# A graph network layer on one core: sorted-table quads closer together, the last node blocks two steps apart, a norm one step later, and a memset on another engine

## The chip, the cores and the metric

The kernel runs on one core of a Trainium2 chip. Its engines work side by side, each through its own list of instructions in order: TensorE (PE) multiplies, VectorE (DVE) and ScalarE (ACT) work on elements, GpSimd (POOL) issues the gathers and scatters whose rows are named by an index (indirect DMAs), SyncE (SP) issues the plain DMAs. They meet at semaphores. The metric is the time of one execution on the device in microseconds (us), the median of several runs; lower is better.

## The reference, cut to what matters

Three layers of message passing over 6250 nodes with 256 features and 100000 edges of three types, in single precision. The edges come sorted by their destination, which is denser at low node numbers. Each edge has 32 attributes, which one matrix turns into its weights; these serve all three layers.

```
ew = edge_attr @ edge_w + edge_b
inv_cnt[i] = 1 / max(number of edges of type i into the node, 1)
for l in range(3):
    residual = x
    msg = relu(x[src] * ew)
    out = 0
    for i in range(3):
        h = segment_sum(msg * (edge_type == i), dst) * inv_cnt[i]
        out = out + h @ weights[l, i]
    out = out + x @ roots[l] + biases[l]
    x = residual + relu(out)
result = layernorm(x_in + x)
```

## The kernel before, in words

The edges are cut into tiles of 128; two tiles are a pair, two pairs a quad. There are 391 pairs. The nodes are cut into 49 blocks of 128 (the last has 106). The names of the blocks are 0 to 48.

Each layer is one list of steps, written out by the function `layer`, whose loop over `it` emits for every step the instructions of several stages, each for a pair that lies some steps ahead. The schedule is manual: what stands earlier in this loop stands earlier in the list of its engine. The list of layer 0 has 391 steps, those of layers 1 and 2 have 414. A step `it` does:

- `gather` (line 1422, POOL): two indirect DMAs fetch the source rows of the pair of step `it + 9` into a quad buffer `xs`, of which there are 8;
- `reduce` (lines 881, 884, 892, PE): the messages of the pair of step `it` are multiplied with one-hot matrices (destination by type) and summed up in a bank of PSUM, `h_p`; `add` (line 932, DVE) later adds a finished bank to the accumulator `acc`;
- `make_ew` (line 820, PE; layer 0 only): the edge weights of the quad five steps ahead, into a PSUM buffer `ew_p`;
- `keep_ew` (layer 0 only): ACT copies the weights of the quad four steps ahead into one of three buffers `keep`. For most quads (line 776) SP writes them to memory for the later layers;
- `weigh` (line 843 on DVE, line 844 on ACT): product of the rows and their weights, then the relu, for the quad three steps ahead;
- the end of a node block (below), and in layer 2 its norm.

**The sorted table.** The first 52 pairs of edges (26 quads) go to a few nodes. In layer 0 their weights are not kept in order: each row is scattered to a place in a table in memory (`zone_table`), sorted by source block and type, from which the later layers read them with plain loads and without a gather. For these quads `keep_ew` (line 770) leaves the four tiles in a list `waiting`, and `gather_pair` calls `scatter` (line 733) after each of its gathers as long as that list has entries. So POOL's list has four scatters between gathers soon after each such quad, and the first of them waits for the copy of line 770. At which steps these quads stand is set by `places_of`: near `ZONE_AT + int(ZONE_SPACE * j)` for quad number j, counted in pairs of the list, rounded up to an even pair. The same places cut the sums of `reduce` (`spans_of`).

**The end of a block.** The function `schedule` gives each block c a step `starts[c]` once all of its sums are there. Blocks 2 to 48 come in this order, with block 0 among them; block 1 is the last of all. Most blocks take two steps per part, the last five (44 to 48, `QUICK = 5`) one step per part (`paces`). With s the start of one of those five: at step s `node_mul` (line 961, PE) multiplies the first type's sum with its weights into the PSUM buffer `o_p`; at s + 1 `node_end` (lines 988 to 992, DVE) adds that to `x_root`, and `node_mul` does the other two types; at s + 2 `node_end` adds those, makes the new rows (line 995) and SP writes them to memory (line 998, `x_mid`), and ACT clears the sums (line 978). There is one buffer `o_p`, so a matmul into it waits until DVE has read the one before. Within a step `node_end` stands ahead of `node_mul`.

**From layer to layer.** The first 6 pairs of the next layer (12 gathers, `gather_early`) are put in POOL's list at steps 388 to 393 of layer 0 and 411 to 416 of layer 1, behind all other gathers of the layer. They read `x_mid`, which block 48's write completes; block 1 is left out of them and added later (`complete`, line 835).

**The norm** (layer 2). When a block is over at step o, `node_end` also makes its mean and variance in `mv` (lines 1001 and 1003, DVE; two buffers each). `deviate` (line 1007, ACT) takes the root at o + 1; `norm` at o + 2 takes the reciprocal (1012) and a product (1013) on DVE, scales the rows on ACT (1014) and writes them out (1015, SP; ACT for block 1).

**Columns of ones.** The quad buffers `xs` have a 257th column of ones, with which line 881 counts edges while it sums. Line 517 sets it once, for all 8 buffers, before layer 0.

Of the kernel before, what the change touches and what calls it, by code (L numbers as in the profile page):

```python
# [442 lines left out]
def ordered_path(ctx, tc, x, attr_laid, A, weights, roots, biases, edge_w, edge_b, out, src, src_i, seg, place_i, consts, x_root,  # L443
# [6 lines left out]
    nc = tc.nc  # L450
    P = 128
    N, D = x.shape
    E = src.shape[0]
    L, R = weights.shape[:2]
    NT = (N + P - 1) // P
# [58 lines left out]

    edge = ctx.enter_context(tc.tile_pool(name="edge", bufs=2))
    all_rows = big.tile([P, ROWS, 2, 2, D + 1], F32, name="xs")
    nc.vector.memset(all_rows.rearrange("p n k i d -> p (n k i) d")[:, :, D:], 1.0)
    rooms = [all_rows[:, n] for n in range(ROWS)]
    wpool = ctx.enter_context(tc.tile_pool(name="wpool", bufs=1))
    o_pool = ctx.enter_context(tc.tile_pool(name="o_p", bufs=1, space=PSUM))  # L520
# [163 lines left out]
    def layer(l, r_sb, b_sb, ats, early, pools):  # L684
# [4 lines left out]
        order, starts, moved, _, _ = schedule(N, E, share, l)  # L689
# [15 lines left out]
        def first_of(p, n):  # L705
            return p == 0 or order[p - 1] // n != order[p] // n
# [302 lines left out]
        def norm(c):  # L1009
            n = min(P, N - c * P)  # L1010
            mv = mvs[c]
            nc.vector.reciprocal(mv[:n, 1:2], mv[:n, 2:3])
            nc.vector.scalar_tensor_tensor(mv[:n, 0:1], mv[:n, 0:1], -1.0, mv[:n, 1:2], op0=ALU.mult, op1=ALU.mult)
            nc.scalar.activation(x_all[:n, c, :], x_all[:n, c, :], AF.Identity, bias=mv[:n, 0:1], scale=mv[:n, 1:2])
            (nc.scalar if c == 1 else nc.sync).dma_start(out[c * P:c * P + n, :], x_all[:n, c, :])
# [10 lines left out]
        over_at = {s + 2 * paces(c, NT): c for s, c in node_at.items()}  # L1026
# [5 lines left out]
        for j, c in enumerate(turns_of):  # L1032
            step = max(3 + int((steps - 110) * (1 - (1 - j / NT) ** 0.5)), max(root_at, default=-1) + 6)
            if j >= roots_in:
                step = max(step, starts[turns_of[j - roots_in]] + 5)
            assert step + 8 <= starts[c]
            root_at[step] = c
        if l > 0:
            for p, u in enumerate(order):
                if u >= ZU:  # L1040
                    _, b, n = lots[u // 2 - ZU // 2]
# [3 lines left out]
        if l == L - 1:  # L1045
            used = {c: s + 1 for s, c in root_at.items()}
            used[1] = max(used[1], FIRST + 1)
            for p, u in enumerate(order):
                if u >= ZU:
                    _, b, n = lots[u // 2 - ZU // 2]  # L1050
                    used.update((c, max(used[c], p - 3)) for c in range(b, b + n))
            for c in turns_of:
                step = max(used[c], max(given_at, default=0) + 2)
                assert step <= starts[c] + 2, (c, step, starts[c])
                given_at[step] = c
        for it in range(-11, max(starts) + 8):
            it_is[0] = it
            def pair(k):
                return order[it + k] if 0 <= it + k < steps else None
# [26 lines left out]
            if l == L - 1 and it in given_at:  # L1086
                c = given_at[it]
# [21 lines left out]
            if pair(3) is not None and pair(3) // 2 == order[-1] // 2:  # L1109
                k = pair(3) % 2  # L1110
# [36 lines left out]
                    node_mul(1, 2)  # L1147
            if it - 1 in over_at and l == L - 1:
                deviate(over_at[it - 1])
            if it - 2 in over_at and l == L - 1:  # L1150
                norm(over_at[it - 2])
            if pair(2) is not None and first_of(it + 2, 2) and pair(2) // 2 != order[-1] // 2:
                one_hot(pair(2) // 2)
            if pair(3) is not None and first_of(it + 3, 2) and pair(3) // 2 == order[-1] // 2:
# [40 lines left out]
SORT_AT = 4  # L1195
SORT_EVERY = 6
ZONE_AT = 114
ZONE_SPACE = 7.5
MIDDLE_AT = 12
LOT_AT = 6  # L1200
LOT_SPACE = 4.5
# [1 line left out]
QUICK = 5  # L1203
# [48 lines left out]
def places_of(N, E):  # L1252

    K = first_pairs(N, E)
    quads = [K + ZONE_AT + int(ZONE_SPACE * j) for j in range(zone_of(N, E) // 2)]
    lots = [K + LOT_AT + int(LOT_SPACE * j + LOT_MORE * j * j) for j in range(len(lots_of(N)))]
# [96 lines left out]
def paces(c, NT):  # L1353

    return 1 if c >= NT - QUICK else 2


def schedule(N, E, share, l):

    P = 128  # L1360
    U = -(-E // (2 * P))
    NT = -(-N // P)
    K = first_pairs(N, E)
    last = last_pairs(N, E)
    spans = spans_in(N, E, l)
    order = order_of(N, E, l)
    added = {s: p + 1 for s, p in stages(N, E, share, l)[2].items()}
    done = []
    for c in range(NT):
        edges = E * min(1.0, (P * (c + 1) / N) ** 0.5)  # L1370
        u = U if c == NT - 1 else min(U, -(-int(edges) // (2 * P)) + 4)
        done.append(max(added[s] for s in spans if K <= s[0] < U and (s[0] < u or s[0] == K)))
    node = lambda e: int(N * min(1.0, max(0.0, e / E)) ** 2)
    least = [node(2 * P * u - ASTRAY) for u in range(U)]
    most = [node(2 * P * u + ASTRAY) for u in range(U)]
    for u in range(last, U):
        least[u] = max(least[u], P)
    moved = done[1] + 1
    ready = max(added[s] for s in spans if s[0] < last or s[0] >= U) + 2
    starts = [None] * NT  # L1380
    step = moved
    for c in range(2, NT):
        if starts[0] is None and ready <= max(done[c] + 2, step + 4):
            step = starts[0] = max(ready, step + 4)
        step = starts[c] = max(done[c] + paces(c, NT), step + 2 + paces(max(c - 1, 2), NT))
    if starts[0] is None:
        step = starts[0] = max(ready, step + 4)
    starts[1] = max(max(added.values()), step + 4)

    for s in spans:  # L1390
        u, p = s[0], added[s]
        if u >= U:
            assert p <= starts[0]
        elif u >= K:
            assert all(p <= starts[c] or least[u] >= P * (c + 1) for c in range(2, NT))
            assert p <= moved or least[u] >= 2 * P
            assert all(p < starts[c] or least[u] >= P * c for c in range(8, NT, 8))
            for b in range(RING // P + 1, (most[u] + WIN - 1) // P + 1):
                assert (moved + 2 if b - RING // P == 1 else starts[b - RING // P] + 4) < p
        else:  # L1400
            assert most[u] <= 2 * P and p <= starts[1] and (p <= starts[0] or u >= last)
    return order, starts, moved, least, most
# [246 lines left out]
```

## Time and profile before

| | |
|---|---|
| median of 3 runs | 3883.04 us (3883.04, 3887.07, 3860.34) |
| profiled execution | 3860.15 us, span of the core 3858.3 us |
| granted clock of TensorE, mean | 0.839 |
| busy share: PE, DVE, ACT, POOL | 68%, 49%, 49%, 55% |
| layer 0, layer 1, layer 2 | about 0 to 1715, 1715 to 2775, 2775 to 3858 us |

The profile shows one execution. Its time is 22.9 us under the median of the three runs and equals the fastest of them. In its rows the time is in us from the start of the span, then come the duration, the engine, the line, the operation and its tiles; what stands in brackets is how long the engine had been idle and what released it. "issue" is idle time in which the engine waited for nothing that the profile shows, "remote" one whose releaser it doesn't know. Where layers begin and end is read from the first gathers and the last sums of each.

### The profile page before, as it was taken

Reading aid. Unit: us, or ns where it says so; the run is one execution under the profiler, and the core shown is the slowest. Engines: PE = TensorE matmul, PEld = TensorE weight load, DVE = VectorE, ACT = ScalarE, POOL = GpSimd, SP = SyncE. Lnnn points to the kernel's source line nnn. Section 1 sums busy time; section 2 is a strip of 40 time slices with the busy share of each in tenths; the row PEclk is TensorE's granted clock in tenths of the full one; section 3 lists DMA queues with packets and bytes.
Section 4 is the critical chain, followed back from the end, with each engine's and each line's share of the span. In section 5 each row is a group of like instructions: output and inputs, shape, how many; then the busy total and the mean of one; then the engine's idle time right before and its main releaser. Section 6 shows DMA issues by size and latency. Waiting matters only on the chain.

```text
span 3858.3 us, 44988 instructions
## 1 busy us (share of the span) xinstructions
PE 2608.3 (68%) x12908; PEld 2006.4 (52%) x12908; DVE 1891.5 (49%) x4217; ACT 1882.9 (49%) x2571; POOL 2141.1 (55%) x2253
## 2 busy tenths in 40 slices
PE   4778665555655655566788777767668687777666
PEld 2445343433433433444666666666556566666655
DVE  5566444443544333443454555544345455555555
ACT  4566444433433333444555554545445555555555
POOL 6666544445444454536666665666566556555663
PEclk8899777777777777788899999888879989988888
DMA  6888444434343343446777666666567666666664
GB/s 197 264 263 262 152 138 139 131 130 135 127 133 122 120 134 119 153 163 204 227 225 236 218 222 210 204 215 215 189 209 240 216 223 223 220 216 210 216 204 151
DMA packets 358717, 730.70 MB, mean 189 GB/s; under 512 B 59082, under 2 KB 215804, under 8 KB 358460
## 3 DMA queue, kind: packets, MB, share of 16 engines
q1 hardware_dynamic: 243840, 426.41, 32.4%
q0 software_dynamic: 107616, 294.11, 25.7%
q10 hardware_dynamic: 7004, 7.19, 0.6%
q8 instruction: 107, 1.75, 0.2%
q14 instruction: 150, 1.23, 0.1%
HBM read 570.03 MB, written 157.46 MB: 189 GB/s over the span
## 4 chain that ended last, share of the span: by engine, by line
PE 35%; issue 21%; another core or an unknown queue 10%; DVE 9%; ACT 4%; DMA 2%; POOL 2%; DVEq 1%; SPq 0%; ACTq 0%; POOLq 0%
PE h_p L892 11%; PE o_p L961 8%; PE h_p L884 6%; PE ew_p L806 3%; DVE xs L843 3%; PE ew_p L820 2%; PE r_p L945 2%; DVE x_root L992 2%; POOL xs L1422 2%; DVE acc L932 2%; DMA xs<-x_mid,src_r 1%; ACT xs L844 1%; DVE oh L860 1%; PE h_p L904 1%
## 5 line engine op out<-in xcount | busy, mean ns | idle before, releaser
L1422 POOL DMA_INDIRECT xs<-x_mid,src_r x1332 | 1266.3, 951 | 812.1 <-issue 389.2
L1422 POOL DMA_INDIRECT xs<-in_x_dram,src_io x770 | 735.4, 955 | 388.9 <-issue 214.8
L892 PE MATMUL h_p<-oh,xs 128*128 128x120 f32 x4720 | 730.8, 305 | 276.4 <-issue 117.8
L843 DVE TENSOR_TENSOR xs<-ew_p,xs 128x1024 f32<-128x1024 f32 x533 | 644.6, 1212 | 511.3 <-ACT keep L776 340.5
L892 PEld LDWEIGHTS h_p<-oh,xs 128*128 128x128 f32 x4720 | 680.6, 214 | 378.9 <-issue 189.7
L844 ACT ACTIVATE xs<-xs 128x1024 f32<-128x1024 f32 x533 | 559.0, 1049 | 475.2 <-DVE xs L843 290.5
L961 PE MATMUL o_p<-w_sb,acc 128*128 128x256 f32 (+1 forms) x1752 | 515.2, 437 | 164.3 <-DVE x_root L992 84.2
L932 DVE TENSOR_TENSOR acc<-h_p,acc 128x240 f32 (+1 forms) x767 | 341.4, 447 | 514.3 <-remote 182.7
L961 PEld LDWEIGHTS o_p<-w_sb,acc 128*128 128x128 f32 (+1 forms) x1752 | 363.3, 219 | 255.2 <-issue 90.4
L776 ACT ACTIVATE keep<-ew_p 128x1024 f32<-128x1024 f32 x170 | 173.4, 1020 | 636.5 <-issue 514.0
L820 PE MATMUL ew_p<-x_root,at 64*128 64x512 f32 x606 | 211.4, 777 | 352.4 <-ACT ew_p L794 182.4
L884 PE MATMUL h_p<-xs,oh 128*120 128x256 f32 x1136 | 310.3, 408 | 62.8 <-DVE acc L932 26.7
L791 ACT ACTIVATE ew_p<-ew_s 128x1024 f32<-128x1024 f32 (+1 forms) x340 | 343.9, 1012 | 15.4 <-DMA ew_s<-ew_all 13.4
L992 DVE SCALAR_TENSOR_TENSOR x_root<-o_p,inv,x_root 128x256 f32<-128x256 f32 (+1 forms) x438 | 210.9, 482 | 284.5 <-remote 137.9
L733 POOL DMA_INDIRECT zone_table<-keep,slot_i x104 | 102.2, 983 | 421.2 <-ACT keep L770 374.3
L884 PEld LDWEIGHTS h_p<-xs,oh 128*120 128x120 f32 x1136 | 216.2, 198 | 113.4 <-issue 37.1
L881 PE MATMUL h_p<-xs,oh 128*120 128x257 f32 x756 | 227.8, 434 | 63.2 <-issue 39.0
L820 PEld LDWEIGHTS ew_p<-x_root,at 64*128 64x128 f32 x606 | 54.4, 218 | 398.3 <-ACT ew_p L794 194.2
L844 ACT ACTIVATE zone<-zone 128x1024 f32<-128x1024 f32 (+1 forms) x78 | 78.7, 1009 | 366.5 <-DVE zone L843 226.9
L843 DVE TENSOR_TENSOR zone<-ew_p,zone 128x1024 f32<-128x1024 f32 (+1 forms) x78 | 90.7, 1163 | 282.5 <-PE ew_p L806 97.4
L881 PEld LDWEIGHTS h_p<-xs,oh 128*120 128x120 f32 x756 | 146.8, 207 | 138.5 <-issue 68.6
L978 ACT ACTIVATE acc<-zero_o 128x768 f32<-128x768 f32 (+1 forms) x150 | 141.3, 942 | 149.5 <-remote 85.0
(184 smaller groups left out, 3136.5 us busy)
## 6 DMA issues: line engine op xcount, KB each, us to landing
ew_s<-ew_all SPq DMA_DIRECT2D x338, 512.0 KB
ew_all<-keep SPq DMA_DIRECT2D x169, 512.0 KB
oh_l<-oh_all SPq DMA_DIRECT2D x338, 120.0 KB
zone<-zone_table SPq DMA_DIRECT2D x72, 516.0 KB
xs<-x_mid,src_r POOLq DMA_INDIRECT x1332
oh_all<-oh_b SPq DMA_DIRECT2D x169, 120.0 KB
zone_table<-blank SPq DMA_DIRECT2D x21, 677.2 KB
x_mid<-x_all SPq DMA_DIRECT2D x98, 128.0 KB
```

The source lines that it names most:

```text
L776: nc.scalar.activation(ew_s[:, :n], ew_ps[q][:, :n], AF.Copy)
L791: nc.scalar.activation(ew_ps[q][:, :n], ew_ss[q][:, :n], AF.Copy)
L820: nc.tensor.matmul(ew_ps[q][:, k].rearrange("p i d -> p (i d)"), at[half, :], ew_sb[half].rearrange("p i d -> p (i d)"), start=False, stop ...
L843: nc.vector.tensor_mul(there, ew_ps[q][:, pairs.start:pairs.stop, :n], there)
L844: nc.scalar.activation(there, there, AF.Relu)
L881: nc.tensor.matmul(h_p[:WK, :D + 1], ohs[u // 2][:, t, :], wide[u // 2][:, u % 2, i, :], start=(i == 0 and first), stop=(i == n - 1 and cl ...
L884: nc.tensor.matmul(h_p[:WK, :D], ohs[u // 2][:, t, :], rows_of(u, i), start=(i == 0 and first), stop=(i == n - 1 and closes(u)), skip_grou ...
L892: nc.tensor.matmul(h_p[:, d * WK:(d + 1) * WK], rows_of(u, i)[:, d * P:(d + 1) * P] if d < DC else full_ones, (ohs if d < DC else oh_bs)[u ...
L932: nc.vector.tensor_tensor(there, h_ps[span][:, :CH * WK].rearrange("p (c r w) -> p c r w", c=CH, r=R), there, op=ALU.add)
L961: nc.tensor.matmul(o_p[:n, j, :], acc[:, d, r, slot:slot + n], w_sb[:, r * DC + d, :], start=(d == 0), stop=(d == DC - 1))
L992: nc.vector.scalar_tensor_tensor(root, o_p[:n, j, :], inv[:n, c, r:r + 1], root, op0=ALU.mult, op1=ALU.add)
L1422: nc.gpsimd.indirect_dma_start(out=xs[:, u % 2, i, :], out_offset=None, in_=x_rows[:, :], in_offset=bass.IndirectOffsetOnAxis(ap=src_i[:, ...
```

## The change

Four edits in three functions and one table of numbers.

```
-    nc.vector.memset(all_rows.rearrange("p n k i d -> p (n k i) d")[:, :, D:], 1.0)
+    nc.gpsimd.memset(all_rows.rearrange("p n k i d -> p (n k i) d")[:, :, D:], 1.0)
...
-            if it - 2 in over_at and l == L - 1:
-                norm(over_at[it - 2])
+            if it - 3 in over_at and l == L - 1:
+                norm(over_at[it - 3])
...
-ZONE_SPACE = 7.5
+ZONE_SPACE = 7.1
...
-        step = starts[c] = max(done[c] + paces(c, NT), step + 2 + paces(max(c - 1, 2), NT))
+        apart = 2 if c > NT - QUICK and step == starts[c - 1] else 4
+        step = starts[c] = max(done[c] + paces(c, NT), step + apart)
```

The first sets the columns of ones on POOL. The second puts `norm` one step later; `deviate` stays. The third moves the quads of the sorted table: before, their steps in the list of layer 0 are 120, 130, 140, 148, 158 and so on to 358, with 19 gaps of ten steps and 6 of eight; after, they are 120, 130, 138, 148, 156 and so on to 348, with 14 gaps of ten and 11 of eight. The list keeps its 391 steps, so ten steps that stood between such quads stand behind the last one. Block 0, which needs their sums, starts at step 354 of layer 0, where it was 364.

The fourth lets each of the blocks 45 to 48 start two steps behind the one before it (three before) if the block before it is the one that was placed last. Their starts follow, with the sums that they need as the other bound:

| blocks 44, 45, 46, 47, 48 | before | after |
|---|---|---|
| layer 0 | 368, 371, 374, 377, 380 | 366, 368, 372, 375, 377 |
| layers 1 and 2 | 388, 392, 396, 399, 402 | 388, 392, 396, 398, 400 |

Where two blocks stand two steps apart, the `node_end` that finishes the first and the first `node_mul` of the second fall in one step. Block 1 keeps its start, 392 and 415. The number of instructions of each line is the same but for the memset. Lines behind 1371 have a number that is one higher after the change: the gathers are line 1423.

POOL's list in layer 0, around the second and third quad of the sorted table, before (128x256 is a gather of one tile, 32128x258 the table into which a tile is scattered):

```order
L1422 DMA xs<-in_x_dram,src_io 128x256 x17
L733 DMA zone_table<-keep,slot_i 32128x258
L1422 DMA xs<-in_x_dram,src_io 128x256
L733 DMA zone_table<-keep,slot_i 32128x258
L1422 DMA xs<-in_x_dram,src_io 128x256
L733 DMA zone_table<-keep,slot_i 32128x258
L1422 DMA xs<-in_x_dram,src_io 128x256
L733 DMA zone_table<-keep,slot_i 32128x258
L1422 DMA xs<-in_x_dram,src_io 128x256 x17
```

The same place after:

```order
L1423 DMA xs<-in_x_dram,src_io 128x256 x17
L733 DMA zone_table<-keep,slot_i 32128x258
L1423 DMA xs<-in_x_dram,src_io 128x256
L733 DMA zone_table<-keep,slot_i 32128x258
L1423 DMA xs<-in_x_dram,src_io 128x256
L733 DMA zone_table<-keep,slot_i 32128x258
L1423 DMA xs<-in_x_dram,src_io 128x256
L733 DMA zone_table<-keep,slot_i 32128x258
L1423 DMA xs<-in_x_dram,src_io 128x256 x13
```

Between the second quad's scatters and the third's stand 17 gathers before and 13 after: two steps, of two gathers each, have gone from between them.

PE's list near the end of layer 1, before (128x256 and 106x256 are `node_mul` of a whole block and of block 48, 120x256 and 128x120 sums of messages, line 904 turns a sum):

```order
L961 MATMUL o_p<-w_sb,acc 128x256 x2
L884 MATMUL h_p<-xs,oh 120x256 x2
L904 MATMUL h_p<-ident_o,h_s 128x120 x2
L961 MATMUL o_p<-w_sb,acc 128x256 x4
L884 MATMUL h_p<-xs,oh 120x256 x4
L961 MATMUL o_p<-w_sb,acc 106x256 x2
L884 MATMUL h_p<-xs,oh 120x256 x2
L961 MATMUL o_p<-w_sb,acc 106x256 x4
L884 MATMUL h_p<-xs,oh 120x256 x4
L904 MATMUL h_p<-ident_o,h_s 128x120 x2
L884 MATMUL h_p<-xs,oh 120x256 x6
```

The same place after:

```order
L961 MATMUL o_p<-w_sb,acc 128x256 x2
L884 MATMUL h_p<-xs,oh 120x256 x2
L961 MATMUL o_p<-w_sb,acc 128x256 x4
L884 MATMUL h_p<-xs,oh 120x256 x2
L904 MATMUL h_p<-ident_o,h_s 128x120 x2
L961 MATMUL o_p<-w_sb,acc 106x256 x2
L884 MATMUL h_p<-xs,oh 120x256 x2
L961 MATMUL o_p<-w_sb,acc 106x256 x4
L884 MATMUL h_p<-xs,oh 120x256 x8
L904 MATMUL h_p<-ident_o,h_s 128x120 x2
L884 MATMUL h_p<-xs,oh 120x256 x6
```

Block 48's six matmuls stand two steps, four sums, sooner: behind the last of them eight sums follow up to the turn of line 904, where there were four.

DVE's list in layer 2 at one norm, before (lines 1012 and 1013 are the norm, 932 adds a sum to `acc`, ISA rows are its loads of a place):

```order
L992 SCALAR_TENSOR_TENSOR x_root<-o_p,inv,x_root 128x256
L1012 RECIPROCAL mv<-mv 128x1
L1013 SCALAR_TENSOR_TENSOR mv<-mv 128x1
L932 ISA
L932 TENSOR_TENSOR acc<-h_p,acc 128x6x40
L924 TENSOR_LOAD place_i
```

The same place after:

```order
L992 SCALAR_TENSOR_TENSOR x_root<-o_p,inv,x_root 128x256
L932 ISA
L932 TENSOR_TENSOR acc<-h_p,acc 128x6x40
L1012 RECIPROCAL mv<-mv 128x1
L1013 SCALAR_TENSOR_TENSOR mv<-mv 128x1
L924 TENSOR_LOAD place_i
```

The two operations of the norm have changed places with one `add`.

## The prediction

> **What bounds the kernel now.** I read the page first: its shares, the granted clock and the chain of work that ended last.
>
> ```profile
> span 3858.3 us, 44988 instructions
> PE 2608.3 (68%) x12908; PEld 2006.4 (52%) x12908; DVE 1891.5 (49%) x4217; ACT 1882.9 (49%) x2571; POOL 2141.1 (55%) x2253
> PEclk8899777777777777788899999888879989988888
> PE 35%; issue 21%; another core or an unknown queue 10%; DVE 9%; ACT 4%; DMA 2%; POOL 2%; DVEq 1%; SPq 0%; ACTq 0%; POOLq 0%
> ```
>
> No engine is busy throughout, and a third of the chain (21% and 10%) is time in which an engine waited for nothing the profile can name. The digits of the clock show where: they sink to 7 between the fifth and the twenty-first slice, inside layer 0. So I cut the span by stages, first all engines, then the ACT half of `weigh` (line 844), of which there is one per quad, or per two steps.
>
> ```profile
> 100.00:400.00 300.00, 238.00 (x995) 148.74 (x996) 184.37 (x482) 191.09 (x259) 182.12 (x192) 0.90 0.80 259
> 400.00:1600.00 1200.00, 687.06 (x3389) 471.61 (x3389) 506.37 (x1299) 470.51 (x589) 571.32 (x595) 0.75 0.40 131
> 1715.00:2775.00 1060.00, 777.04 (x3986) 652.83 (x3985) 515.00 (x946) 537.97 (x746) 643.35 (x678) 0.88 0.67 214
> ```
>
> ```profile
> 100.00:400.00 300.00, 51.57 (x49) 0.90 0.80 259
> 400.00:1584.00 1184.00, 128.13 (x122) 0.75 0.40 131
> 1584.00:1700.00 116.00, 14.96 (x15) 0.85 0.48 156
> 1716.00:2764.00 1048.00, 217.85 (x209) 0.88 0.67 215
> ```
>
> A step costs 300/98 = 3.06 us before the quads of the sorted table, 1184/244 = 4.85 us among them, 116/30 = 3.87 us behind the last one, and 1048/418 = 2.51 us in layer 1. Among those quads no engine is busy for 60% of the time (the columns are PE, its weight loads, DVE, ACT, POOL). What the quads do there is told by the scatters (line 733) and by one cycle of the timeline.
>
> ```profile
> L733 POOL DMA_INDIRECT zone_table<-keep,slot_i x104: 979/981/1002, 403.0 to 1583.9; - x104
>   ACT keep L770: 374.3, 25
> ```
>
> ```profile
> 864.18 0.98 POOL L733 DMA_INDIRECT zone_table<-keep,slot_i  x1 [13.96 <-ACT keep L770]
> 902.54 0.98 POOL L733 DMA_INDIRECT zone_table<-keep,slot_i  x1 [13.39 <-ACT keep L770]
> 930.32 0.94 POOL L1422 DMA_INDIRECT xs<-in_x_dram,src_io  x1 [0.30 <-issue]
> 933.67 1.02 ACT L776 ACTIVATE keep<-ew_p 128x1024 f32<-128x1024 f32 x1 [24.36 <-issue]
> 949.48 0.98 POOL L733 DMA_INDIRECT zone_table<-keep,slot_i  x1 [12.75 <-ACT keep L770]
> 1431.31 0.98 POOL L733 DMA_INDIRECT zone_table<-keep,slot_i  x1 [12.94 <-ACT keep L770]
> 1479.37 0.98 POOL L733 DMA_INDIRECT zone_table<-keep,slot_i  x1 [23.07 <-issue]
> 1528.48 0.98 POOL L733 DMA_INDIRECT zone_table<-keep,slot_i  x1 [14.64 <-ACT keep L770]
> 1576.21 0.98 POOL L733 DMA_INDIRECT zone_table<-keep,slot_i  x1 [17.74 <-ACT keep L770]
> ```
>
> POOL stands still 13 to 18 us before a quad's first scatter until ACT has copied that quad's weights (374.3 us over 25 quads, 15 each). With that wait it loses its lead of gathers, and it wins it back in one run without a pause, here from 902.54 to 931.26. ACT's next copy, idle for 24.36 us for no reason that the profile names, starts 2.4 us after the run's end. I read this as news that comes late while POOL runs back to back; the rows show the coincidence, not the cause. So each quad brings a hold, and holds, not an engine, bound this stage.
>
> **The change, part by part.** The sum is made against the profiled execution, 3860.15 us; the median of the runs shown is 3883.04, so what comes out is added to that.
>
> *The quads' places.* From the first scatter of the first quad (403.0) to that of the last (1576.21) are 1173.2 us for 238 steps. The first scatters of all 26 quads (first and last above) cut this into 19 cycles of ten steps with a mean of 48.7 us and 6 of eight with 41.4. Of the latter the cycle from 864.18 to 902.54 (38.4) is one of the first four (36.9 to 41.5, mean 38.7), and that from 1431.31 to 1479.37 (48.1) one of the last two (mean 46.7). A long cycle beside each: 902.54 to 949.48 is 46.9, 1479.37 to 1528.48 is 49.1. Two steps less save 7.3 us by the means, 3.65 each, about the price of a step outside the table. The hold itself, 41.4 − 8 × 3.65 = 12 us, stays, and so do its 26 instances. After the change there are 14 long cycles and 11 short: 14 × 48.7 + 11 × 41.4 = 1137.2, which is 36.0 less. The ten steps are not gone; they stand behind the last quad, for 10 × 3.87 = 38.7 us by the nearest row (30.6 by the row ahead of the quads). So +2.7 net. Counted by place, with nine of the short cycles where they were 38.7 and two where they were 46.7, it is 14 × 48.7 + 9 × 38.7 + 2 × 46.7 = 1123.5, 49.7 less, and −11 net. I take the middle, −4; the bounds are below with the rivals.
>
> *Blocks 44 to 48 sooner.* At the layers' ends, the write of block 48, the first and the last of the twelve early gathers, and the next work of DVE:
>
> ```profile
> 1691.84 0.30 SPq L998 DMA_DIRECT2D x_mid<-x_all  x1
> 1696.86 0.95 POOL L1422 DMA_INDIRECT xs<-x_mid,src_e  x1 [29.30 <-PE h_p L881]
> 1710.64 0.95 POOL L1422 DMA_INDIRECT xs<-x_mid,src_e  x1 [0.30 <-issue]
> 1714.11 0.53 DVE L932 TENSOR_TENSOR acc<-h_p,acc 128x360 f32 x1 [13.86 <-remote]
> 2753.96 0.25 SPq L998 DMA_DIRECT2D x_mid<-x_all  x1
> 2758.95 0.96 POOL L1422 DMA_INDIRECT xs<-x_mid,src_e  x1 [16.82 <-PE h_p L884]
> 2772.75 0.95 POOL L1422 DMA_INDIRECT xs<-x_mid,src_e  x1 [0.30 <-issue]
> 2776.10 0.48 DVE L992 SCALAR_TENSOR_TENSOR x_root<-o_p,inv,x_root 128x256 f32<-128x256 f32 x1 [3.74 <-remote]
> ```
>
> The first early gather starts 5.02 us after the write was issued in layer 0 and 4.99 us in layer 1: too alike for chance, so I take it that the write's landing starts them. Then POOL runs for 14.7 us, and DVE's last `add` of layer 0 comes 2.5 us after that run (1711.59 to 1714.11), idle for 13.86 us. The write now comes three steps sooner in layer 0 and two in layer 1: at most 3 × 3.87 + 2 × 2.51 = 16.6 us. It won't be had in full, since a run that comes sooner also falls on steps that ran free of it before: what it held for 13.86 us at the end it will hold, in part, ahead of the end. I take a third, −5.5, with −16.6 and +5 (all that is held is then late by a further two steps of 2.51) as its ends. Layer 2 has no early gathers and gains nothing here.
>
> By the Trainium skill, page "DMA: Bandwidth & Descriptors", section "Anatomy of one DMA — SWDGE (gpsimd) path", a transfer takes about 2.0 us and a part for its bytes, an estimate of 2.3 us for these 128 KB (its fit is for transfers issued by GpSimd; this one is SP's). The rows have 5.0 us from write to gather; by the page the write would have landed 2.7 us before the gather began, and something else would start it, so that this term would be nothing. I go by the two rows and keep that as a rival.
>
> *Two steps apart.* Six times, twice in each layer, a block's first `node_mul` now waits in its own step for the DVE end of the block before.
>
> ```profile
> L961 PE MATMUL o_p<-w_sb,acc 128*128 128x256 f32 (+1 forms) x1752 | 515.2, 437 | 164.3 <-DVE x_root L992 84.2
> 1689.21 1.23 DVE L843 TENSOR_TENSOR xs<-ew_p,xs 128x1024 f32<-128x1024 f32 x1 [0.38 <-ACT keep L776]
> 1690.35 0.99 DVE L992 SCALAR_TENSOR_TENSOR x_root<-o_p,inv,x_root 106x256 f32<-106x256 f32 x2
> ```
>
> Line 961 waited 84.2 us for line 992 over some 147 blocks, 0.6 us each; the two operations of line 992 take 0.99 us. Six new waits cost between nothing (PE has the step's sums to do meanwhile) and 6 × 2.2 = 13 us (0.99 and the 1.23 of a `weigh` that stands ahead of it on DVE); behind PE's wait stand only its own sums of the next step. I take +3.
>
> *The norm.* The waits before its first operation, in layer 2:
>
> ```profile
> L1012 DVE RECIPROCAL mv<-mv x49: 129/155/166, 2936.4 to 3852.3; 128x1 f32<-128x1 f32 x48, 106x1 f32<-106x1 f32 x1
>   ACT mv L1007: 6.4, 8
>   ACT xs L844: 4.5, 5
>   issue: 3.2, 6
> ```
>
> A step more lets the root of line 1007 end first: at most 6.4 + 3.2 = 9.6 us of DVE's idle time go. The 4.5 us are a `weigh` of ACT ahead of line 1007 and may stay. DVE is off the path in part, so I take −4, with −9.6 and +1 as ends: one `add`, which now stands ahead, can be late, but then delays only an output that SP writes. At the layer's end nothing stands between, and block 1's norm comes when it did.
>
> *The memset.*
>
> ```profile
> 0.74 0.20 POOL masks.py:197 MEMSET ident_o<- 128x128 f32 x1 [0.29 <-POOLq L1632]
> 21.50 0.09 DVE L517 MEMSET xs<- 128x32 f32 x1
> 21.98 0.95 POOL L1422 DMA_INDIRECT xs<-in_x_dram,src_io  x1 [2.56 <-PE ew_p L820]
> ```
>
> DVE loses 0.09 us, POOL gets some 0.2, inside the 2.56 us in which it idles before the first gather of the list. If that cover were gone it would cost those 0.2 us: nothing.
>
> The sum: −4 − 5.5 + 3 − 4 = −10.5 us; the profiled execution would be 3849.7, the median 3872.5.
>
> **The rivals.**
>
> *Short cycles are cheap everywhere.* The first four of the six were 38.7 us, and the last two may owe their 46.7 to their neighbours: 1479.37's scatter waited 23.07 us on "issue", not on ACT. Then eleven take 425.7, the stage 1107.5 (65.7 less), the ten steps behind cost 34.6 by the mean of both rows, and with −6.5 from the other parts it is −37.6: 3845. In its best case, all at 36.9 and the steps at 3.06 us, it is −55 and with the rest 3821.
>
> *Short cycles are no shorter: slower.* After a scatter POOL runs for 28.7 us (902.54 to 931.26) and then stands 13 us. Eight steps may not outlast the run; the next wait then comes before the lead is won back, and the cycle costs what the last two did, 46.7 us. Then the stage takes 14 × 48.7 + 11 × 46.7 = 1195.5, 22.3 more, and the ten steps come on top: +61, with the rest +54.5: 3937. The change turns to a loss where a short cycle exceeds (1173.2 − 681.8 − 38.7 + 6.5)/11 = 41.7 us. Against it speak the first four, for it the last two.
>
> *The early gathers don't start with the write.* The view names PE's sums as their releaser (29.30 and 16.82 us), not a DMA. If it is right, or the page is on the landing, they start when they did, the layers end when they did, and −5 is left: 3878.
>
> *The order changes and nothing else.* If the holds fill up whatever is taken out (a block sooner, a norm later), the time is that of before, 3883.
>
> **How the numbers follow.** Forecast 0.40, cheap short cycles 0.23, no early start 0.15, nothing 0.12, dear short cycles 0.10. One per cent is 39 us, about what a measurement of this kernel can tell from no change: the three runs alone differ by 27. Faster by that much (below 3844) is half of the cheap case, 0.12, and a low end of the forecast with the start of the layers at its bound, 0.07: with one for the scatter of the runs 0.20. Slower by that much needs short cycles above 45.3 us: 0.09. The rest is 0.71. The range goes from 3826, near the best of the cheap case, to 3908, where the short cycles have used up some 44 us each; outside lie the far ends of both, 0.15 to 0.2.
>
> **What would show it.** In the changed kernel's profile: the last scatter at about 1550 us (1583.9 before), the means of cycles of eight and ten steps near 41 and 49, layer 0's end at 1715 less 5 to 12; above 45 for a short cycle the slower rival holds, below 39 the cheap one. The first early gather 5.0 us behind block 48's write, both some 10 us sooner against the last `add` of layer 0; if that gap grows, the write did not start it. Line 1012's wait for line 1007 gone; line 961's wait for line 992 up by about 3 us. The granted clock among the quads still near 0.75. Wrong would be a change in layer 1's or layer 2's middle, where no list has changed, or a stage of quads whose holds are fewer or shorter than 26 times 12 us.

## The result, and the profile after

| | before | after |
|---|---|---|
| median of 19 runs, us | 3877.26 (3857.02 to 3891.85) | 3851.97 (3838.32 to 3873.02) |
| profiled execution: span, us | 3858.3 | 3850.0 |
| granted clock | 0.839 | 0.835 |

The ratio of after to before is 0.9944, 95% interval 0.9926 to 0.9962: the changed kernel is 21.7 us faster, with an interval of 14.7 to 28.7. (The ratio is that of the means; the medians are 25.3 us apart.) That lies within one per cent, as forecast as the likeliest, and in the range (3826 to 3908). The forecast was 10.5 us: the sign was right and the size half of what came.

The two profiled executions differ by 8.3 us only, since that of before was among its fastest runs (the prediction noted it). So parts are compared below over all profiles that share a list, not from this pair alone.

The first view is the ACT half of `weigh` by windows of the changed kernel (columns: window, length, busy time and count, clock, DMA share, GB/s), with the scatters and three of them in a row from the timeline:

```profile
400.00:1584.00 1184.00, 125.50 (x121) 0.75 0.41 130
1584.00:1700.00 116.00, 17.81 (x18) 0.90 0.56 181
1716.00:2764.00 1048.00, 216.41 (x208) 0.88 0.67 213
```

```profile
L733 POOL DMA_INDIRECT zone_table<-keep,slot_i x104: 976/977/1675, 405.5 to 1546.1; - x104
  ACT keep L770: 368.9, 25
```

```profile
849.77 0.98 POOL L733 DMA_INDIRECT zone_table<-keep,slot_i  x1 [14.94 <-ACT keep L770]
891.86 0.98 POOL L733 DMA_INDIRECT zone_table<-keep,slot_i  x1 [17.14 <-ACT keep L770]
942.24 0.98 POOL L733 DMA_INDIRECT zone_table<-keep,slot_i  x1 [16.00 <-ACT keep L770]
```

The last scatter is over at 1546 (before 1584). GpSimd waits as long before the first scatters as before (368.9 us, 374.3), the clock among the quads is the same 0.75, and layer 1 has the same pace. From 849.77 to 891.86 is a cycle of eight steps (42.1 us), the one behind it has ten (50.4). Over all first scatters of this profile the 11 short cycles have a mean of 40.6, the 14 long ones of 49.1 (before 41.4 and 48.7).

What the other engines do in GpSimd's wait before the scatter at 849.77, and in the run that follows it (columns: window, length, then busy time and count of PE, its weight loads, DVE, ACT and POOL, clock, DMA share, GB/s):

```profile
834.83:849.77 14.94, 13.56 (x77) 9.07 (x77) 12.35 (x32) 11.37 (x16) 0.00 (x1) 0.87 0.48 169
849.77:874.73 24.96, 12.68 (x65) 8.62 (x63) 9.81 (x26) 6.55 (x8) 19.17 (x20) 0.83 0.43 132
```

TensorE is busy for 91% of this wait and 51% of this run. Over 25 quads it is 82% of the waits (15 us each) and 47% of the runs (27 us each, counted from the first scatter until GpSimd stands still for 1 us).

The layers' ends: block 48's write, the first and last early gather, and the `add` behind them, in layer 0 and in layer 1.

```profile
1676.25 0.30 SPq L998 DMA_DIRECT2D x_mid<-x_all  x1
1680.99 0.94 POOL L1423 DMA_INDIRECT xs<-x_mid,src_e  x1 [22.26 <-DMA at_q<-in_attr_laid_dram]
1694.75 0.95 POOL L1423 DMA_INDIRECT xs<-x_mid,src_e  x1 [0.30 <-issue]
1698.33 0.53 DVE L932 TENSOR_TENSOR acc<-h_p,acc 128x360 f32 x1 [6.77 <-issue]
1706.33 0.32 SPq L998 DMA_DIRECT2D x_mid<-x_all  x1
2738.83 0.25 SPq L998 DMA_DIRECT2D x_mid<-x_all  x1
2743.94 0.96 POOL L1423 DMA_INDIRECT xs<-x_mid,src_e  x1 [16.73 <-PE h_p L884]
2757.70 0.95 POOL L1423 DMA_INDIRECT xs<-x_mid,src_e  x1 [0.30 <-issue]
2761.11 0.41 DVE L932 TENSOR_TENSOR acc<-h_p,acc 128x240 f32 x1 [13.21 <-remote]
2768.07 0.32 SPq L998 DMA_DIRECT2D x_mid<-x_all  x1
```

The early gathers follow the write by 4.74 and 5.11 us (5.02 and 4.99 before), and the `add` again starts about 2.5 us after the end of GpSimd's run (1695.70 to 1698.33; 2758.65 to 2761.11). From the first early gather to that `add` it is 17.3 us in layer 0, where it was 17.25: the write did not come sooner against it, as the prediction's signs had it, for the `add` moves with the run.

The waits before the norm's first operation, and from the timeline the memset with the first gather and, at the end of layer 1, the first `node_mul` of blocks 47 and 48, each two steps behind another block:

```profile
L1012 DVE RECIPROCAL mv<-mv x49: 152/154/164, 2923.5 to 3843.7; 128x1 f32<-128x1 f32 x48, 106x1 f32<-106x1 f32 x1
...
  ACT mv L1007: 0.4, 1
```

```profile
21.30 0.15 POOL L517 MEMSET xs<- 128x32 f32 x1 [1.91 <-PE ew_p L820]
22.05 0.95 POOL L1423 DMA_INDIRECT xs<-in_x_dram,src_io  x1 [0.59 <-issue]
...
2719.50 1.13 PE L961 MATMUL o_p<-w_sb,acc 128*128 128x256 f32 x4 [0.23 <-issue]
...
2730.71 2.04 PE L961 MATMUL o_p<-w_sb,acc 128*106 128x256 f32 x4 [6.01 <-DVE x_root L992]
```

The 14.1 us before line 1012 are down to 0.4. Of the six new handovers from DVE to TensorE these two cost 0.23 and 6.01 us, the other four next to nothing. Line 961's waits for line 992 over the whole span rose from 84.2 to 113.2 us, but most of that lies far from the new handovers, and with the blocks alone they are 81.6. The memset takes 0.15 us on GpSimd, which stood idle there, and the first gather starts 0.07 us later than before.

### The profile page after: what moved, and what is told of

Its sections match the earlier page's. It is cut to its first block, busy times and chain, and to the rows that moved or that the text cites. A ratio compares the mean times of both kernels' runs of the same rounds, so it can differ in the third digit from the quotient of the medians.

```text
span 3850.0 us, 44982 instructions
## 1 busy us (share of the span) xinstructions
PE 2610.6 (68%) x12908; PEld 2010.0 (52%) x12908; DVE 1892.2 (49%) x4216; ACT 1883.4 (49%) x2571; POOL 2135.4 (55%) x2254
## 5 line engine op out<-in xcount | busy, mean ns | idle before, releaser
L961 PE MATMUL o_p<-w_sb,acc 128*128 128x256 f32 (+1 forms) x1752 | 524.9, 444 | 170.7 <-DVE x_root L992 113.2
L961 PEld LDWEIGHTS o_p<-w_sb,acc 128*128 128x128 f32 (+1 forms) x1752 | 371.4, 224 | 273.0 <-DVE x_root L992 78.1
L733 POOL DMA_INDIRECT zone_table<-keep,slot_i x104 | 102.5, 986 | 414.2 <-ACT keep L770 368.9
```

The costliest lines, as they stand in the source:

```text
L961: nc.tensor.matmul(o_p[:n, j, :], acc[:, d, r, slot:slot + n], w_sb[:, r * DC + d, :], start=(d == 0), stop=(d == DC - 1))
```

## The experiments

The theory: the quads' places carry the gain, because GpSimd loses its lead at each first scatter and wins it back in a run that holds the others. The rivals: the last blocks or the norm carry it, or the stage of the quads is bound by something else than that lead. Ratios are to the kernel before, in us against its median in the same comparison (3891.8, 3876.1, 3838.4 and 3880.2 in the four that were made).

### The quads' places alone

```
-ZONE_SPACE = 7.5
+ZONE_SPACE = 7.1
```

> Only the quads of the sorted table move (the table spacing 7.1 in place of 7.5), the rest is as before. Theory: the ten steps moved behind the table cost less there (about 2.5 us each by the profile of the changed kernel, 24.8 us more from the last scatter to the layer's end) than they cost between quads (3.6 to 4 us), so this edit alone gives most of the gain: 10 to 16 us faster (ratio 0.996 to 0.997). Rival: the steps' price is the same on both sides and the gain is that of the blocks two steps apart: then 0 to 4 us (ratio 0.999 to 1.000).

Ratio 0.9929 (0.9907 to 0.9951), 27.6 us faster (19 to 36). The scatters:

```profile
L733 POOL DMA_INDIRECT zone_table<-keep,slot_i x104: 976/977/1673, 406.5 to 1529.8; - x104
```

From the first scatter to the last are 1123.3 us. The edit alone gives as much as the whole change, and more than the 10 to 16 us that were expected.

### The last blocks alone

```
-        step = starts[c] = max(done[c] + paces(c, NT), step + 2 + paces(max(c - 1, 2), NT))
+        apart = 2 if c > NT - QUICK and step == starts[c - 1] else 4
+        step = starts[c] = max(done[c] + paces(c, NT), step + apart)
```

> Only the last five blocks stand two steps apart. Theory: the twelve early gathers start sooner at the ends of layers 0 and 1, less what the late steps are held by them: 3 to 8 us faster (ratio 0.998 to 0.999), and the gap from block 48's write to the first early gather stays near 5 us. Rival: this edit is the one that carries the gain, 15 to 22 us (ratio 0.994 to 0.996); second rival: six new waits of TensorE for VectorE eat it up, 0 or slower.

Ratio 0.9996 (0.9976 to 1.0015): 1.6 us faster, between 9 faster and 6 slower. The writes of blocks 48 and 1 at the end of layer 1 in this run, and in the kernel before:

```profile
2765.75 0.25 SPq L998 DMA_DIRECT2D x_mid<-x_all  x1
2794.90 0.32 SPq L998 DMA_DIRECT2D x_mid<-x_all  x1
```

```profile
2753.96 0.25 SPq L998 DMA_DIRECT2D x_mid<-x_all  x1
2777.07 0.32 SPq L998 DMA_DIRECT2D x_mid<-x_all  x1
```

From the one write to the other it is 29.2 us, before 23.1. In layer 1 block 48 is two steps sooner, but the layer ends no sooner against it: what was won ahead of the write, 6 us, is given back behind it. From block 1's write of layer 0 to that of layer 1 it is 1070.8 us, in the run with the norm alone 1069.6. In layer 0 most is kept: the stretch behind the write is 30.8 us (29.3 before), and from the last scatter to block 1's write it is 126.9 us, where 137.2 (before) and 133.8 (the norm alone) go by with the old blocks. These are single profiles; the ratio doesn't tell the 7 to 10 us from nothing.

### Fewer early gathers at a layer's end

Built on the changed kernel, to see what gives it back:

```
-FIRST = 6
+FIRST = 4
```

> The changed kernel with 4 early pairs (8 early gathers) in place of 6 (12). Theory of the hold at a layer's end: the sums that finish late wait for the end of GpSimd's run, which is now 10 us and not 15, so the stretch from block 48's write to block 1's (30.1 us in layer 0, 29.2 in layer 1 of the changed kernel) falls by 3 to 5 us in both; what the two pairs that are gathered later cost shows behind it. In all 0 to 8 us faster than the changed kernel (ratio 0.992 to 0.994). Rival: that stretch is set by the sums and matmuls themselves: it stays at 29 to 30 us and the time is the changed kernel's or longer (ratio 0.994 to 0.998).

Ratio 0.9923 (0.9892 to 0.9955); the interval overlaps that of the changed kernel (0.9944, 0.9926 to 0.9962). The end of layer 1:

```profile
2736.20 0.25 SPq L998 DMA_DIRECT2D x_mid<-x_all  x1
2741.32 0.95 POOL L1423 DMA_INDIRECT xs<-x_mid,src_e  x1 [18.88 <-PE h_p L884]
2750.08 0.95 POOL L1423 DMA_INDIRECT xs<-x_mid,src_e  x1 [0.30 <-issue]
2752.91 0.41 DVE L932 TENSOR_TENSOR acc<-h_p,acc 128x240 f32 x1 [7.65 <-remote]
2759.64 0.32 SPq L998 DMA_DIRECT2D x_mid<-x_all  x1
```

Counted from its own start the run ends 5.0 us sooner, and the `add` comes 5.6 us sooner: it starts 1.9 us after the run (2751.03), and DVE's wait falls from 13.21 to 7.65. From write to write it is 23.4 us (29.2), in layer 0 23.8 (30.1). So the run of early gathers sets that stretch, as the theory had it, by 5.8 and 6.3 us where 3 to 5 were expected. How much of the 6 us per layer end remains in the whole can't be told from this ratio.

### The norm alone, and the change without it

```
-            if it - 2 in over_at and l == L - 1:
-                norm(over_at[it - 2])
+            if it - 3 in over_at and l == L - 1:
+                norm(over_at[it - 3])
```

> Only the norm stands one step later. Theory: VectorE's waits before the reciprocal go (14 us in the profile before, 0.4 us in that after), of which a third was on the path: 3 to 5 us faster (ratio 0.9987 to 0.9993). Rival: those waits were hidden, no change (ratio 1.000).

Ratio 0.9973 (0.9953 to 0.9993), 10.5 us faster (3 to 18), where 3 to 5 were expected. The other way round, the changed kernel with `it - 2` put back:

> The changed kernel with the norm where it was before, two steps after a block's start, all else changed. Theory: the norm is worth what its waits on the path are, 3 to 5 us, so this is 3 to 5 us slower than the changed kernel (ratio to before 0.995 to 0.996 where the changed kernel has 0.9944). Rival, from the run with the norm alone (10 us faster): ratio 0.997.

Ratio 0.9944 (0.9922 to 0.9965), the same as with the whole change. Its waits are back:

```profile
L1012 DVE RECIPROCAL mv<-mv x49: 129/157/166, 2894.2 to 3794.5; 128x1 f32<-128x1 f32 x48, 106x1 f32<-106x1 f32 x1
  ACT mv L1007: 7.5, 10
  issue: 5.7, 9
```

The waits come and go with the edit, as expected. Its price is not settled: 3 to 18 us by the one comparison and 0 with some 11 to either side by the other. Both leave room for the predicted 4. The profiles don't decide it either: layer 2, where alone the edit acts, takes from block 1's write in layer 1 to the end 1078.4 us with the norm alone, and in the same comparison 1078.2 (the places alone) and 1088.5 (the blocks alone) with the norm as before.

### The scatters seven steps later

The changed kernel; a quad's scatters may only be taken from the list seven steps after its weights were copied, and the copies of the quads have a buffer of their own:

```
+            if waiting and waiting[0][4] <= it_is[0]:
+                there, q, k, i, _ = waiting.pop(0)
...
+                there = early_pool.tile([P, 2, 2, D + 2], F32, name="keep_z", bufs=1)
...
+                waiting.extend((there, q, k, i, it_is[0] + 7) for k in range(2) for i in range(2))
...
-KEEP = 3
+KEEP = 2
```

> The changed kernel, with the four scatters of each quad put seven steps later in GpSimd's list, so that GpSimd does not have to wait for the copy of that quad's weights; these copies get one buffer of their own and the other copies keep two in place of three. Theory of the hold: GpSimd keeps its lead of gathers, the 15 us in which it stands still before each first scatter go (369 us in all), and so do the run behind it and the hold of ScalarE in it; of some 12 us per quad a good half goes: 150 to 300 us faster than before (ratio 0.92 to 0.96). Rival: the stage is bound by something else in it (the scatters themselves, SyncE's transfers, the two buffers), and the time stays within 30 us of the changed kernel (ratio 0.985 to 1.00).

Ratio 0.9252 (0.9226 to 0.9279), 291 us faster. Of the scatters' row and the waits before them (the longest one; no wait for line 770 is left):

```profile
L733 POOL DMA_INDIRECT zone_table<-keep_z,slot_i x104: 977/977/1002, 414.1 to 1284.1; - x104
  issue: 28.0, 92
```

The same 850 us among the quads, all engines (PE, weight loads, DVE, ACT, POOL; then clock, DMA share, GB/s), in the changed kernel and in this one:

```profile
420.00:1270.00 850.00, 481.59 (x2374) 330.33 (x2375) 366.92 (x957) 335.34 (x421) 403.41 (x422) 0.75 0.41 131
```

```profile
420.00:1270.00 850.00, 626.49 (x3105) 428.13 (x3104) 471.72 (x1209) 439.21 (x548) 524.39 (x547) 0.83 0.54 170
```

With the waits gone every engine does 29 to 31% more in the same time, and the clock rises from 0.75 to 0.83. The first to last scatter takes 870 us (1141), so 369 us of waits less make the stage 271 us shorter, 11 us per quad. The stage was bound by the lost lead: by the waits together with the runs that they set off.

### Four steps later, with the common buffers

The same with `+ 4`, and the buffers as in the changed kernel:

> The changed kernel with a quad's scatters four steps later in GpSimd's list (seven in the run before), with the three common buffers as they were. Theory: of the seven steps of lead that GpSimd loses four are kept, so a good half of the gain of seven steps (288 us against before, 270 against the changed kernel) comes: 140 to 190 us faster than before (ratio 0.95 to 0.965). Rival: it is the buffer of their own that made the difference there, not the place of the scatters: ratio 0.99 to 1.00.

Ratio 0.9538 (0.9495 to 0.9581), 179 us faster. The wait before the scatters:

```profile
  ACT keep L770: 165.4, 25
```

Four steps take 203 of the 369 us of waits and 157 of the 269 us that seven steps gain over the changed kernel (21.7 of both are the change's). So the place of the scatters is enough without the buffer; whether the buffer has a share in the gain of seven steps is not tested.

### Six quad buffers

The changed kernel with a smaller lead to lose:

```
-ROWS = 8
+ROWS = 6
```

> The changed kernel with 6 quad buffers in place of 8, so that GpSimd's lead of gathers over TensorE is at most 12 steps, not 16, and what it loses at a first scatter is 3 steps, not 7. Theory: the run behind a scatter is eight gathers (10 us) shorter, the wait before it 10 us shorter, and with them the hold: about 6 to 8 us less per quad, 150 to 200 us faster than before in layer 0 (ratio 0.95 to 0.96), if the smaller lead costs nothing in layers 1 and 2. Rival: the hold does not come from the run but from the scatters themselves: layer 0 as in the changed kernel, and the time not lower, or higher by what layers 1 and 2 lose (ratio 0.995 to 1.03).

Ratio 0.9338 (0.9305 to 0.9371), 257 us faster, more than expected. The first scatters of three quads:

```profile
867.90 0.98 POOL L733 DMA_INDIRECT zone_table<-keep,slot_i  x1 [4.07 <-ACT keep L770]
905.27 0.98 POOL L733 DMA_INDIRECT zone_table<-keep,slot_i  x1 [2.62 <-ACT keep L770]
936.60 0.98 POOL L733 DMA_INDIRECT zone_table<-keep,slot_i  x1 [2.95 <-ACT keep L770]
...
  ACT keep L770: 98.5, 25
```

The wait falls from 15 to 4 us on average (98.5 us over 25 quads), the run behind it from 27 to 18 us, the long cycles' mean to 39.0 and that of the short to 33.8. Layers 1 and 2 lost nothing in this profile (1062 and 1076 us from one last write to the next and to the end; 1062 and 1082 in the changed kernel). Less prefetch made the kernel faster.

### Quads six steps apart

The changed kernel with half of its gaps at six steps:

```
-ZONE_SPACE = 7.1
+ZONE_SPACE = 5.0
```

> The changed kernel with the table's spacing at 5.0: 12 gaps of six steps and 13 of eight between its quads (before: 6 of eight and 19 of ten), the last quad at step 296, 52 steps more behind it than in the changed kernel. Theory: a step between two quads costs 4.2 us and one behind the last 3.0 us, so cycles of six take about 32 us, the stage 12 x 32 + 13 x 40.4 = 909, 215 less than the changed kernel's 1124, the 52 steps 156 behind: 55 to 60 us faster than the changed kernel, 80 us faster than before (ratio about 0.98). Rival: below eight steps GpSimd's run fills the cycle and cycles of six cost as much as those of eight, 40: stage 1010, no faster than before (ratio 1.00 to 1.01).

Ratio 0.9712 (0.9668 to 0.9756), 112 us faster, where 80 were expected. Four first scatters, six, eight and six steps apart:

```profile
853.02 0.98 POOL L733 DMA_INDIRECT zone_table<-keep,slot_i  x1 [15.23 <-ACT keep L770]
881.47 0.98 POOL L733 DMA_INDIRECT zone_table<-keep,slot_i  x1 [8.50 <-ACT keep L770]
922.37 0.98 POOL L733 DMA_INDIRECT zone_table<-keep,slot_i  x1 [12.81 <-ACT keep L770]
950.85 1.01 POOL L733 DMA_INDIRECT zone_table<-keep,slot_i  x1 [8.53 <-ACT keep L770]
```

The 12 cycles of six steps have a mean of 28.0 us (25.5 to 29.9), the 13 of eight 40.5. From ten to eight steps a cycle loses 8.5 us (49.1 and 40.6 in the changed kernel), from eight to six 12.5: the hold is not a fixed sum per quad. In six steps GpSimd can't win back a lead of seven, and its wait before the next scatter is 8 us (5.6 to 10.0), where behind eight steps it is 11 to 20.

### The spacing when the hold is gone

The kernel with scatters seven steps later, with the spacing of before (7.5):

> The kernel with the scatters seven steps later, with the spacing of before (7.5) in place of 7.1. Theory: the spacing gains 27 us in the kernel before because a step between quads carries a share of the hold; with the hold gone a step costs much the same on both sides, so the spacing is worth little: within 12 us of the run with 7.1 (ratio to before 0.922 to 0.929). Rival: the spacing is worth the same 25 to 30 us here, since what it shortens is something else (the work of sorting, the cut of the sums): ratio 0.931 to 0.933.

Ratio 0.9277 (0.9239 to 0.9314), against 0.9252 with 7.1 in another comparison: 10 us, with some 17 to either side. By the profiles block 1's write of layer 0 comes at 1433.7 us with 7.5 and at 1430.7 with 7.1, 3 us apart, where the spacing alone moved it from 1732.5 (the run with the norm alone, old places) to 1694.5. From the first to the last scatter it is 907.9 us with 7.5 and 870.0 with 7.1, from there to block 1's write 112.8 and 146.5: a step costs 3.8 us between quads and 3.4 behind them. That is as the theory has it. But the two profiles are of different comparisons, whose kernels before differ by 0.4%, 6 us here, and the ratio by itself doesn't exclude the rival.

### Six buffers and scatters four steps later; five buffers

```
-ROWS = 8
+ROWS = 6
...
+                waiting.extend((there, q, k, i, it_is[0] + 4) for k in range(2) for i in range(2))
...
-KEEP = 3
+KEEP = 5
```

> The changed kernel with 6 quad buffers, scatters four steps later and 5 common buffers for the copies of weights. With 6 buffers GpSimd leads by at most 12 steps, of which a scatter in its old place takes 3, so four steps later it should not wait at all. Theory: the holds of the quads go as with seven steps and 8 buffers, and every other run of GpSimd without a pause is shorter too: layer 0 as there (1431 us) or up to 20 us shorter, the whole 3570 to 3600 (ratio 0.92 to 0.93). Rival: with the smaller lead gathers come late once the scatters stand between them: slower than the run with 8 buffers and seven steps (ratio 0.93 to 0.95).

Ratio 0.9201 (0.9166 to 0.9236): 3528.97 us where the kernel before has 3838.41, 307 us faster. This is the fastest version found that sums rightly, if by little (0.9252, 0.9226 to 0.9279, with seven steps and eight buffers), 7.5% faster than the changed kernel by the quotient of the ratios. Layer 0 ends with block 1's write at 1410 us (1676 in the run without the norm's move, of the same comparison; 1431 with eight buffers and seven steps, of another).

With `ROWS = 5`:

> The changed kernel with 5 quad buffers: GpSimd leads by at most 10 steps, one more than the 9 at which its list puts a gather, so at a first scatter it loses one step. Theory of the lost lead: the wait before a first scatter nearly goes (98 us over 25 quads with 6 buffers, 369 with 8) and the stage shrinks by a further 25 to 50 us from 918 (ratio 0.92 to 0.93) unless a lead of ten steps is too short for the gathers. Rival, that it is: TensorE waits for rows in all layers, and layers 1 and 2 grow by 30 us or more each (ratio 0.94 to 0.97).

Ratio 0.9156 (0.9115 to 0.9197). This one sums wrong rows: with five buffers the gather of step `it + 9` takes, in odd steps, the buffer that `reduce` reads in step `it`, and the gather stands ahead of it in the list. So its lead isn't the one that was expected, and its time is only a hint that a short lead costs layers 1 and 2 nothing (1051 and 1063 us).

## Why the prediction was right and where it was wrong

**The hold of the quads** was read rightly: scatters wait, the lead goes, a run wins it back and holds the others. Taking away the lost lead, by place (seven steps, four steps) or by size (six buffers), shortens the stage from first to last scatter from 1140.6 us to 870, 981 and 926. By the busy shares of TensorE, 82% in the waits and 47% in the runs, it is the run that costs more. In each of the changed kernel's 25 runs ACT's next copy of weights behind it starts 1.5 to 5.8 us after the run's end, in 14 of them after ACT has stood idle for 16 us or more; with six buffers and shorter runs it never stands idle so long (15.7 us at most). So the late news goes with the run. Why the engines hear late no run here shows.

**The price of the quads' places is the term that was mis-sized most**: −4 us were predicted, −27.6 (19 to 36) measured. Two parts of it were off.

The first is the stage, which the middle that I took made 43 us shorter (36.0 by the means, 49.7 by place). The runs of one comparison have 1123.3 us with the new places and 1192.3, twice, with the old. Over four profiles with the new places (the changed kernel, the places alone, without the norm, with fewer early gathers) the first to last scatter takes 1140.6, 1123.3, 1114.5 and 1126.3 us, over three with the old ones 1180.9, 1192.3 and 1192.4: 62 us less, or 58 when the four comparisons are scaled to one median before. The pair of the first comparison alone has 40, as predicted, so this part shows only over several profiles. Five long cycles that became short ones explain 37 of the 62 by the old means (49.0 and 41.6), much as the prediction had it. The rest is that all cycles are shorter in the new list, the short ones by 1.5 us (17 us in all) and the long ones by 0.6 (8 us), and for that no run gives a reason. "The hold itself [...] stays" took two cycle lengths for a rule: at six steps a cycle has 28.0 us, which leaves 28.0 − 6 × 3.65 = 6 us of hold, not 12.

The second is the ten steps behind the table at 3.87 us each. From the last scatter to block 1's write it is 137.2 and 133.8 us with the old places and the old blocks, 164.7 with the new places alone: 29 us for ten steps, 2.9 each. The window that I chose (1584 to 1700) begins at the last scatter, so it holds the run behind it, until 1602, which the change moves but doesn't add to. In the changed kernel that run is over ahead of the window, and the same window has 116/36 = 3.2 us per step; the row ahead of the quads (3.06) was the nearer one. −62 and +29 make −33, the profiles' version of the 27.6.

The rival nearer to this part was "Short cycles are cheap everywhere" (0.23), with −65.7 + 34.6 = −31. Its mechanism came in part only: the short cycles have a mean of 40.6 us in the changed kernel and 39.3 to 40.3 in the other three, between its 38.7 and the 41.4 of the forecast. "Short cycles are no shorter" fell with the same means.

**Blocks 44 to 48**: −5.5 + 3 were predicted and −1.6 (−9 to +6) came. That the write starts the early gathers was right (4.74 and 5.11 us, wherever the write stands), so the rival without an early start fell, and the estimate of 2.3 us for a landing from the Trainium skill ("DMA: Bandwidth & Descriptors", section "Anatomy of one DMA — SWDGE (gpsimd) path") did not describe what this write takes to its reader's start. The trace's records of single packets tell the landing: the 106 rows of 1024 bytes that block 48 writes (106 KB, not 128) move from 0.8 until 3.5 to 3.8 us after the issue, and the gather starts 1.2 to 1.5 us after the last of them, in both layers, before and after. That the sooner run would take back a part was right: in layer 1, where the stretch behind the write grew by the whole 6 us, it took all, in layer 0 little. TensorE's new waits, +3 in the sum, were 6.3 us for the six in the changed kernel, nearly all of it block 48's in layer 1.

**The norm**: its waits went as said; the price, 4 predicted, is not settled beyond 0 to 18. **The memset**: nothing, as said.

The three parts alone add up to 40 us (some 14 to either side, from their own intervals of 7 to 9), the whole to 21.7 (14.7 to 28.7). Whether the parts take something from each other or the single ones came out high is left open. So the time inside the range is in part luck: the places alone gave 24 us more than their term, the blocks and the norm together nothing that can be told apart from theirs, and the whole only 11 us more than the sum.

## What to carry to other kernels

A wait that makes a prefetching queue fall back to the place of its consumer need not cost by itself: here the other engines worked on through most of it, and the time was lost in the run behind it. Look what the queue does right after its wait. A hold measured at two spacings isn't a constant; vary the spacing once more, or take away the lead, before its price is carried over. And more prefetch buffers can cost time where each loss of lead is followed by a run that fills them.

## What the runs showed that was not expected

Fewer quad buffers, 6 for 8, made the changed kernel 6.1% faster (0.9338 over 0.9944), with a shorter wait at each first scatter (4 us for 15) and a shorter run behind it (18 us for 27). And the same list's stage of quads differs by 11 us between profiles of two comparisons (1180.9 and 1192.3), half of what the change moved in all; a pair of single profiles would have put the gain at 8 us.
